# Macaron block on one core: row maxima of three heads moved into the feed-forward, their turns later, score banks apart

## Chip, cores and metric

The kernel runs on one core of one Trainium2 chip. The metric is the device time of one execution in microseconds (us). Three runs took 3427.9, 3429.25 and 3438.38 us, median 3429.25 us. Engines are named as in the profile: PE is TensorE, PEld its weight load, DVE VectorE, ACT ScalarE, POOL GpSimd, SP the queue that issues most transfers. A bank is one of the eight parts of PSUM, the memory that PE writes its results to; a bank holds 128 x 512 numbers of 32 bits.

## What is computed

Four sequences (B = 4) of T = 1024 rows and D = 512 columns pass through half a feed-forward, attention, and half a feed-forward again. Cut to what matters:

```python
def ffn(x):                                # H = 2048
    gate, up = split(x @ ternary(w_gate_up).T)
    h = silu(gate) * up
    h = h * rsqrt(mean(h * h) + eps)
    return h @ ternary(w_proj).T

def attention(x):                          # 32 query heads, 8 key heads, 16 wide
    Q, K, V = heads of x @ Wq.T + bq, x @ Wk.T + bk, x @ Wv.T + bv
    Q, K = rope(Q), rope(K)
    w = softmax(Q @ K.T / sqrt(16))        # four query heads share a key head
    return (w @ V) @ Wo.T + bo

x = x + 0.5 * ffn(layernorm(x))
x = x + attention(layernorm(x))
x = x + 0.5 * ffn(layernorm(x))
```

The softmax subtracts each row's maximum. The kernel finds these maxima in a pass of its own, before the scores are made a second time for the exponential.

## The kernel before

**Stages.** The work of the four sequences is pipelined. After a first part that prepares weights, each b = 0 to 3 has a feed-forward stage (FFN b), an attention stage (att b), and between att b and the next FFN a short stage of projections. FFN b doesn't work on sequence b alone: it takes three blocks of 512 rows, from feed-forwards that are due, last halves of older sequences ("z" blocks, whose rows are stored) and first halves of newer ones. A last FFN of two blocks ends the kernel. All stages touched here are under a manual schedule: each engine carries out its instructions in the order in which the program writes them.

**The feed-forward chunk** (`chunks`, L312). A block of 512 rows has 16 chunks of 128 hidden columns, so FFN b has 48 chunks; hc is the chunk's number in its block, n in the stage. A chunk runs in this order:

- `hidden` (L199): ACT widens the next weights (L100); PE makes `gu` twice in eight matmuls each (L211); ACT silu (L221); DVE `h` (L223); POOL `sq` and `acc` (L231, L235), the squares for the norm; ACT `high` (L237). `rest()`, called later, has DVE make `low` = h - high (L239).
- `project` (L251): `po` of the chunk two earlier, first for two of the four row tiles; then the call to attention, which is the subject here (see below); then the other two row tiles.
- After a block's last chunk: `factors` (L259) sums the squares on PE, POOL raises them to the power -0.5 (`inv`), DVE halves that (`half`, L277). `end` (L280) then adds `po` times `half` onto x (L288), which empties the four `po` banks; the first two x in one chunk, the other two in the next. It falls at hc = 1 and 2 of the next block, since `project` lags by two. At the stage's end all four x stand in a row.
- `rest()`; at even hc from 4 to 10 DVE normalises a row tile for the next block, with the root of its variance from POOL, and PE turns it one chunk later; steps noted for this hc (`later`, loads of x among them).

**The maxima.** Attention needs, for each of its 8 groups g (four query heads and one key head), 64 maxima; one is a 128 x 512 tile of scores, made by two matmuls of 32 rows each (`sm`, L1079) and reduced along its columns by DVE (`pm`, L1088). Four such, one from each head, run side by side on the four row groups of PE; I call this a four. The feed-forward takes one four in a chunk at most. `early` (L1133) decides it by a share of the stage: EARLY = 188 of a b's 512 maxima are done in FFN b, one four in every chunk from n = 2 (n = 5 for b = 0) to 47, less in total where the stage begins late: 184 for b = 1 to 3 and 172 for b = 0. The rest are done in attention, where each of the 128 steps takes three of them beside two pairs of score tiles, and some steps four (`more`, L1219 and L1236): 19 steps for b = 0 and 7 for each other b.

**The turn.** When a group's 64 maxima are there, `subtract_maxima` (L1097) collects them and puts a function `turn` on a list: PE transposes the maxima (`pmT`, L1113), DVE copies them (`mrow`, L1115), POOL writes them to memory (`d_m`, L1117), and for g = 0 POOL at once loads them back in another layout with four transfers (`mT`, L1130), which wait for `d_m` to land. The `early` call of the next chunk runs it, just ahead of that chunk's four. For b = 1 to 3 these are chunks 18 and 34, for b = 0 chunks 21 and 37. Chunk 18 and 34 (hc = 2) are also those in which the second half of the last block's `end` runs.

**Banks.** In the feed-forward tag `gu` has four banks (0 to 3), shared by `gu`, maxima, `pmT`, `pq` and the turned tiles; `po` has four (4 to 7, the four row tiles in 4, 7, 6 and 5). In attention the scores `s` have two pairs, banks 0 and 1 and banks 2 and 3; the maxima `sm` have 4, 6 and 5, the output `o` has 7. A bank that changes hands waits for the last reader of what was there.

Of the kernel before, what the change touches and what calls it, by code (L numbers as in the profile page):

```python
# [36 lines left out]
def tile_macaron_block(  # L37
# [103 lines left out]
    class FeedForward:  # L141
# [10 lines left out]
        def __init__(self, blocks, label, beside=None, begin=1):  # L152
            self.blocks, self.label, self.beside, self.begin = blocks, label, beside, begin
            self.order = [(k, hc) for k in range(len(blocks)) for hc in range(HC)]
            self.inputs, self.pos, self.accs, self.weights = {}, {}, {}, {}
            self.narrow = {}
            self.later = []
            self.first = tc.tile_pool(name=f"x{label}", bufs=1, reuse_waits="tile")
            self.even = self.first.__enter__()

# [98 lines left out]
        def factors(self, k):  # L259

            label = f"{self.label}_{k}"
            pq = self.ps.tile([P, 4], F32, tag="gu", name=f"pq_{label}")
            for i in range(4):
                for n, acc in enumerate(self.accs[k]):
                    nc.tensor.matmul(
                        pq[:, i : i + 1],
                        lhsT=acc[:, i * P : (i + 1) * P],
                        rhs=ones,
                        start=(n == 0),
                        stop=(n == len(self.accs[k]) - 1),  # L270
                    )
            ms = small.tile([P, 4], F32, tag="ms", name=f"ms_{label}")
            nc.vector.tensor_scalar(ms, pq, 1.0 / H, RMS_EPS, ALU.mult, ALU.add)
            inv = small.tile([P, 4], F32, tag="inv", name=f"inv_{label}")
            inverse_root(inv, ms, 4)
            half = small.tile([P, 4], F32, tag="half", name=f"half_{label}")
            nc.vector.tensor_scalar(half, inv, 0.5, None, ALU.mult)  # L277
            return half

        def end(self, k, half, some=range(4)):  # L280
# [31 lines left out]
        def chunks(self):  # L312
            last = len(self.order) - 1
            due, ends = [], []
            for n, (k, hc) in enumerate(self.order):
                if self.beside is not None:
                    places.piece()
                parts, rest = self.hidden(k, hc)
                if ends:
                    self.end(*ends.pop(), [2, 3])  # L320
                due.append((k, hc, parts))
                behind = due.pop(0) if len(due) > self.LAG else None
                if behind is not None:
                    self.project(*behind, [0, 1])
                if n == last:
                    rest()
                if self.beside is not None:
                    self.beside(self.ps, (n - self.begin) / (last - 1 - self.begin))
                if behind is not None:
                    self.project(*behind, [2, 3])  # L330
                    if behind[1] == HC - 1:
                        half = self.factors(behind[0])
                        self.end(behind[0], half, [0, 1])
                        ends.append((behind[0], half))
                if n < last:
                    rest()
                if k + 1 < len(self.blocks) and 4 <= hc < 12 and hc % 2 == 0:
                    for turn in self.normalize(k + 1, [hc // 2 - 2], self.wp, self.ps, "gu"):
                        self.later.append((hc + 1, turn))
                for step in [step for step in self.later if step[0] == hc]:  # L340
                    self.later.remove(step)
                    step[1]()

            for i in range(4):
                for behind in due:
                    self.project(*behind, [i])
                if i == 1:
                    half = self.factors(k)
            self.end(k, half)
            for _, step in self.later:  # L350
                step()
# [516 lines left out]
    class Attention:  # L868
# [18 lines left out]
        TOTAL = HKV * ITEMS * G  # L887
        READY = (HKV - 1) * STEPS - 5
        FIRST = 3
        EARLY = (3 * ITEMS - 1) * G  # L890

        def __init__(self, b):
            self.b = b


            self.d_q = dram.tile([D, 2, T], F32, tag="d_q", name=f"d_q_{b}", bufs=2)
            self.d_k = dram.tile([2, KV, 2, T], F32, tag="d_k", name=f"d_k_{b}", bufs=2)
            self.d_o = dram.tile([HQ, 2, HD, T], F32, tag="d_o", name=f"d_o_{b}", bufs=2)
            self.aT, self.after, self.when = {}, [], 0
            self.counts, self.turns = [0] * G, [0] * HKV  # L900
            self.pm, self.mT, self.mrows = {}, {}, {}
            self.early_rows = None
            self.rows, self.xTs, self.made = {}, {}, {}
            self.turning = []

        def weights_in(self):
            aux = places.at["out", self.b][2].bitcast(F32)
# [156 lines left out]
        def maxima(self, j, ps, bufs, passes):  # L1064

            g, n = divmod(self.counts[j], self.ITEMS)
            self.counts[j] += 1
            i, half = divmod(n, 2)
            q, *k = places.at["m", self.b, g]
            if g not in self.pm:  # L1070
                self.pm[g] = ring.tile([P, NT, G, 2], F32, tag="pm", name=f"pm_{self.b}_{g}")
            pm = self.pm[g]
            tag = "sm" if bufs < 4 else "gu"
            s = ps.tile([P, 512], F32, tag=tag, name=f"sm_{self.b}_{g}_{j}_{n}", bufs=bufs)
            at = slice(j * SLOT, (j + 1) * SLOT)

            def step(part):
                if part < 2:
                    nc.tensor.matmul(  # L1079
                        s,  # L1080
                        lhsT=q[at, i * P : (i + 1) * P],
                        rhs=k[part][at, half * 512 : (half + 1) * 512],
                        start=(part == 0),
                        stop=(part == 1),
                    )

            def end():
                nc.vector.tensor_reduce(pm[:, i, j, half : half + 1], s, AX.X, ALU.max)  # L1088
                self.turns[g] += 1
                if self.turns[g] == G * self.ITEMS:  # L1090
                    self.subtract_maxima(g, ps, bufs)
                    places.done(("m", self.b, g))

            passes.append(step)
            return end

        def subtract_maxima(self, g, ps, bufs):  # L1097

            b = self.b
            m = small.tile([P, NT, G], F32, tag="m", name=f"m_{b}_{g}", bufs=2)  # L1100
# [5 lines left out]
                mst[:, :, 1, :].bitcast(F32R), by_head, mst[:, :, 0, :], ALU.subtract  # L1106
            )
            rows = G * 2 * NT
            tag = "sm" if bufs < 4 else "gu"

            def turn():
                pt = ps.tile([P, 512], F32, tag=tag, name=f"pmT_{b}_{g}", bufs=bufs)
                nc.tensor.transpose(pt[:rows, :P], mst.rearrange("p j r i -> p (j r i)"), ident)  # L1113
                mrow = small.tile([rows, P], F32R, tag="mrow", name=f"mrow_{b}_{g}", bufs=2)
                nc.vector.tensor_copy(mrow, pt[:rows, :P])  # L1115
                self.mT[g] = dram.tile([rows, P], F32, tag="d_m", name=f"d_m_{b}_{g}", bufs=HKV)
                nc.gpsimd.dma_start(self.mT[g], mrow.bitcast(F32))  # L1117
                if g == 0:
                    self.maxima_in(g, ring, 1)
# [13 lines left out]
        def early(self, ps, share):  # L1133

            for at, kind, g in (
                (0.0, "m", 1),
                (0.3, "m", 2),
                (0.5, "s", 0),  # L1140
                (0.7, "m", self.FIRST),
                (0.8, "s", 1),
            ):
                if share >= at:
                    places.load((kind, self.b, g))
            if self.turning:
                self.turning.pop(0)()
            if sum(self.counts) + G <= min(share, 1.0) * self.EARLY:
                passes, ends = [], []
                for e in range(G):  # L1150
                    ends.append(self.maxima(sum(self.counts) % G, ps, 4, passes))
                together(passes, ends)

        def heads(self, keep):
# [6 lines left out]
        def run(self, keep, wp, ps):  # L1161
# [3 lines left out]
            def scores(g, qh, kc, pair, passes):  # L1165

                name = f"{b}_{g}_{qh}_{kc}_{pair}"
                s = ps.tile([P, 2, 512], F32, tag="s", name=f"s_{name}", bufs=2)
                keys, queries = slice(kc * P, (kc + 1) * P), slice(qh * 512, (qh + 1) * 512)
                q, *k = places.at["s", b, g]  # L1170

# [50 lines left out]
            for n in range(HKV * self.STEPS):  # L1222
# [26 lines left out]
                if late is not None:  # L1249
                    weigh(*late)  # L1250
                if turn is not None:
                    turn()
                late = g, qh, kc, es
            weigh(*late)
            places.done(("s", b, HKV - 2))
# [48 lines left out]
    def stage(b):  # L1304
        return FeedForward(
            blocks[b],
            f"{b}",
            beside=at[b].early if b < B else None,
            begin=1 if b > 0 else 4,
        )  # L1310

# [57 lines left out]
```

## Time and profile before

The profiled execution took 3426.07 us, its span is 3424.3 us, and the mean granted clock of PE is 0.983. Starts and lengths of stages by the windows of the trace, in us:

| stage | from | to | length | PE busy |
|---|---|---|---|---|
| FFN 0 | 314.2 | 636.1 | 321.9 | 316.3 |
| att 0 | 636.1 | 976.0 | 339.9 | 332.2 |
| FFN 1 | 1060.3 | 1385.1 | 324.8 | |
| att 1 | 1385.1 | 1718.2 | 333.1 | |
| FFN 2 | 1802.1 | 2121.9 | 319.8 | |
| att 2 | 2121.9 | 2454.9 | 333.0 | |
| FFN 3 | 2539.9 | 2867.2 | 327.3 | |
| att 3 | 2867.2 | 3197.7 | 330.5 | |
| FFN 4 | 3237.3 | end | 187.0 | |

A line of a timeline has the start, the length of the group, the engine, the source line, the operation, output<-inputs, shapes and how many instructions the group holds; in brackets stands the idle time of that engine just before, and what ended it. A line of a window has its bounds, its length, then busy time and count of PE, PEld, DVE, ACT and POOL, the granted clock of PE (1 is full speed), the busy share of the DMA engines and GB/s.

### The profile page before, as it was taken

The numbers are of one execution on the slowest core, as the hardware profiler recorded it, in microseconds if no ns is written. First come the engines' busy times: TensorE is split into PE (matmuls) and PEld (weight loads), VectorE is DVE, ScalarE is ACT, GpSimd is POOL, SyncE is SP. The second block draws the span as 40 slices with busy tenths as digits, with TensorE's granted clock in tenths as the row PEclk, the third lists the DMA queues.
The fourth block names the chain that finished last, engine by engine and source line by source line (L and its number), as shares of the span: only waits on it lengthen the run. The fifth ranks groups of instructions, "written<-read, shape, count | busy, mean of one in ns | idle before, by whom it ended". The sixth has DMA issues, their size and how long they took to land. (4 is left out here: it accounts for less than half of the span.)

```text
span 3424.3 us, 57120 instructions
## 1 busy us (share of the span) xinstructions
PE 3312.7 (97%) x22744; PEld 2147.2 (63%) x22744; DVE 2181.3 (64%) x3626; ACT 1765.4 (52%) x2346; POOL 950.3 (28%) x927
## 2 busy tenths in 40 slices
PE   5998999999999999999999999999999999999999
PEld 4777777544467777444477776444577775444687
DVE  7965666677636666777366666777256666775243
ACT  5742333577733333687713334778523335787343
POOL 2653343100123333100043333000243332010244
PEclk8999999999999999999999999999999999999999
DMA  3533222122323223123132221232231221322111
GB/s 117 157 97 103 61 76 79 40 94 91 105 60 97 78 65 101 57 99 101 65 89 81 88 79 56 75 98 91 74 106 52 78 91 54 96 92 77 32 45 56
DMA packets 211691, 278.47 MB, mean 81 GB/s; under 512 B 27616, under 2 KB 156640, under 8 KB 211424
## 3 DMA queue, kind: packets, MB, share of 16 engines
q1 hardware_dynamic: 201632, 263.26, 24.7%
q0 software_dynamic: 9792, 11.56, 1.4%
q8 instruction: 179, 2.93, 0.4%
q14 instruction: 88, 0.72, 0.1%
HBM read 216.01 MB, written 58.72 MB: 80 GB/s over the span
## 5 line engine op out<-in xcount | busy, mean ns | idle before, releaser
L1088 DVE TENSOR_REDUCE pm<-sm 128x1 f32<-128x512 f32 x2048 | 1284.6, 683 | 371.0 <-PE sm L1079 367.2
L1187 ACT ACTIVATE e<-s 128x1024 f32<-128x1024 f32 x1024 | 997.5, 1022 | 324.0 <-PE s L1176 321.2
L1079 PE MATMUL sm<-p_m,p_m 32*128 32x512 f32 x4096 | 769.2, 440 | 22.0 <-DVE pm L1088 11.4
L211 PE MATMUL gu<-xT,guT 128*128 128x512 f32 x1792 | 710.3, 396 | 13.3 <-ACT guT L100 12.5
L211 PE MATMUL gu<-xL,guT 128*128 128x512 f32 x1792 | 703.6, 393 | 0.3 <-DVE xL L139 0.3
L1176 PE MATMUL s<-p_s,p_s 32*128 32x512 f32 x4096 | 679.7, 437 | 0.0
L1176 PEld LDWEIGHTS s<-p_s,p_s 32*128 32x128 f32 x4096 | 317.4, 185 | 450.5 <-ACT e L1187 427.1
L1197 PE MATMUL o<-e,vs 128*32 128x512 f32 x4096 | 553.8, 613 | 1.8 <-ACT e L1187 1.8
L1079 PEld LDWEIGHTS sm<-p_m,p_m 32*128 32x128 f32 x4096 | 354.9, 185 | 122.3 <-DVE h L223 54.8
L1176 PE MATMUL s<-mT,ones_r 2*128 2x512 f32 x2048 | 417.3, 398 | 2.8 <-DMA mT<-d_m 2.8
L231 POOL TENSOR_TENSOR sq<-h 128x512 f32<-128x512 f32 x210 | 218.7, 1042 | 708.2 <-DVE h L223 708.0
L211 PEld LDWEIGHTS gu<-xT,guT 128*128 128x128 f32 x1792 | 340.0, 190 | 90.3 <-ACT guT L100 14.2
L221 ACT ACTIVATE sg<-gu 128x512 f32<-128x512 f32 x224 | 134.1, 599 | 497.1 <-PE gu L211 497.1
L223 DVE TENSOR_TENSOR h<-sg,gu 128x512 f32<-128x512 f32 x224 | 153.7, 686 | 368.9 <-PE gu L211 350.9
L211 PEld LDWEIGHTS gu<-xL,guT 128*128 128x128 f32 x1792 | 340.1, 190 | 70.2 <-DVE xL L139 0.7
L251 PE MATMUL po<-w_pT,high 128*128 128x512 f32 x896 | 371.9, 415 | 0.6 <-DVE x L288 0.6
L251 PE MATMUL po<-w_pT,low 128*128 128x512 f32 x896 | 351.8, 393 | 0.1
L237 ACT CAST high<-h 128x512 fp32r<-128x512 f32 x224 | 139.0, 620 | 342.1 <-DVE h L223 320.9
L235 POOL TENSOR_TENSOR acc<-acc,sq 128x512 f32<-128x512 f32 x205 | 276.4, 1348 | 16.0
L100 ACT CAST guT<-g 128x512 fp32r<-128x512 bf16 x448 | 274.8, 613 | 8.2 <-ACT guT L100 5.8
L251 PEld LDWEIGHTS po<-w_pT,high 128*128 128x128 f32 x896 | 168.3, 188 | 99.4 <-issue 65.5
L1176 PEld LDWEIGHTS s<-mT,ones_r 2*128 2x128 f32 x2048 | 198.5, 186 | 31.6 <-DMA mT<-d_m 4.5
(147 smaller groups left out, 3060.9 us busy)
## 6 DMA issues: line engine op xcount, KB each, us to landing
g<-d_guT SPq DMA_DIRECT2D x448, 128.0 KB
p_m<-d_k SPq DMA_DIRECT2D x56, 512.0 KB
p_s<-d_k SPq DMA_DIRECT2D x56, 512.0 KB
d_o<-oT SPq DMA_DIRECT2D x64, 256.0 KB
p_m<-d_q SPq DMA_DIRECT2D x28, 512.0 KB
p_s<-d_q SPq DMA_DIRECT2D x28, 512.0 KB
x<-in_L_attn_x_dram SPq DMA_DIRECT2D x32, 256.0 KB
w<-in_L_ffn_w_gate_up_dram SPq DMA_DIRECT2D x32, 256.0 KB
```

The costliest lines, as they stand in the source:

```text
L100: nc.scalar.copy(w, t)
L211: nc.tensor.matmul(pg, lhsT=self.weights[k, hc][part][:, c, :], rhs=xp[:, c, :], start=(c == 0 and low == 0), stop=(c == DC - 1 and low == 1),
L223: nc.vector.tensor_tensor(h, sg, gu[1], ALU.mult)
L231: nc.gpsimd.tensor_tensor(sq, h, h, ALU.mult)
L235: nc.gpsimd.tensor_tensor(acc, acc, sq, ALU.add)
L237: nc.scalar.copy(high, h)
L251: nc.tensor.matmul(self.pos[k][i], lhsT=h[:, i * P : (i + 1) * P], rhs=w_pT[hc], start=(hc == 0 and n == 0), stop=(hc == HC - 1 and n == 1),)
L1079: nc.tensor.matmul(s, lhsT=q[at, i * P : (i + 1) * P], rhs=k[part][at, half * 512 : (half + 1) * 512], start=(part == 0), stop=(part == 1),)
L1088: nc.vector.tensor_reduce(pm[:, i, j, half : half + 1], s, AX.X, ALU.max)
L1176: nc.tensor.matmul(s[:, e, :], lhsT=k[part][at, keys] if part < 2 else ones_r[at, :], rhs=(q if part < 2 else self.mrows[g])[at, queries], ...
L1187: nc.scalar.activation(w, s, AF.Exp, scale=1.0 / HD**0.5)
L1197: nc.tensor.matmul(o[j * SLOT : (j + 1) * SLOT, :], lhsT=vs[:, kc, g, :], rhs=es[j // 2][:, j % 2, :], start=(kc == 0), stop=(kc == NT - 1),)
```

## The change

- The feed-forward takes all 192 maxima of groups 0, 1 and 2 (EARLY = 192, 48 fours) in every FFN b < 4, and attention the other 320. There is one four in every chunk from n = `begin` (1, or 4 for b = 0) to n = 46 and none in the last chunk, n = 47. What is short of 48 is made up by a second four at the end of some chunks, behind `rest()` and the `later` steps: chunks 14 and 30 for b = 1 to 3; 14, 30, 46, 42 and 40 for b = 0.
- No attention step takes a fourth maximum any more.
- A waiting turn runs at the end of a chunk with hc = 3 or 13 and no longer in `early`: group 0's in chunk 19, group 1's in chunk 35. Group 2's turn runs in attention's step 0, as before.
- The root takes 4 times the mean square, so that POOL's result is `half` itself, and DVE's copy (16 instructions in the whole kernel) is gone.
- The two pairs of score banks have tags of their own, `s0` and `s1`, used in turn. By the built order `s0` has banks 0 and 1, the maxima 2, 4 and 3, `s1` 5 and 6, `o` 7. At attention's start the first scores and the first maximum thus use former `gu` banks; the second maximum waits for the first x of the block's end, the second pair of scores for the last.

```diff
+            short = Attention.EARLY // G - (len(self.order) - 1 - begin)
+            spare = [n for n, (k, hc) in enumerate(self.order[:-1]) if hc == 14]
+            spare += [len(self.order) - n for n in (6, 8, 10, 4, 12)]
+            self.twice_in = spare[:short] if beside is not None else []
...
-            nc.vector.tensor_scalar(ms, pq, 1.0 / H, RMS_EPS, ALU.mult, ALU.add)
-            inv = small.tile([P, 4], F32, tag="inv", name=f"inv_{label}")
-            inverse_root(inv, ms, 4)
+            nc.vector.tensor_scalar(ms, pq, 4.0 / H, 4.0 * RMS_EPS, ALU.mult, ALU.add)
             half = small.tile([P, 4], F32, tag="half", name=f"half_{label}")
-            nc.vector.tensor_scalar(half, inv, 0.5, None, ALU.mult)
+            inverse_root(half, ms, 4)
...
-                if self.beside is not None:
-                    self.beside(self.ps, (n - self.begin) / (last - 1 - self.begin))
+                if self.beside is not None and n < last:
+                    self.beside.early(self.ps, (n - self.begin) / (last - 1 - self.begin))
...
+                if n in self.twice_in:
+                    self.beside.four(self.ps)
+                if self.beside is not None and self.beside.turning and hc in (3, 13):
+                    self.beside.turning.pop(0)(self.ps, 4)
...
-        EARLY = (3 * ITEMS - 1) * G
+        EARLY = FIRST * ITEMS * G
...
-            if self.turning:
-                self.turning.pop(0)()
-            if sum(self.counts) + G <= min(share, 1.0) * self.EARLY:
+            if share >= 0.0:
+                self.four(ps)
+
+        def four(self, ps):
+
+            if sum(self.counts) < self.EARLY:
                 passes, ends = [], []
-                for e in range(G):
-                    ends.append(self.maxima(sum(self.counts) % G, ps, 4, passes))
+                for j in range(G):
+                    ends.append(self.maxima(j, ps, 4, passes))
                 together(passes, ends)
...
-                s = ps.tile([P, 2, 512], F32, tag="s", name=f"s_{name}", bufs=2)
+                s = ps.tile([P, 2, 512], F32, tag=f"s{self.turn_of_s}", name=f"s_{name}")
+                self.turn_of_s = 1 - self.turn_of_s
```

More of the change, by code (lines that the diff above doesn't have):

```diff
@@ L904, in __init__ @@
             self.turning = []
+            self.turn_of_s = 0
         def weights_in(self):
@@ L1090, in end @@
                 if self.turns[g] == G * self.ITEMS:
-                    self.subtract_maxima(g, ps, bufs)
+                    self.subtract_maxima(g)
                     places.done(("m", self.b, g))
@@ L1095, in maxima, with subtract_maxima @@
             return end
-        def subtract_maxima(self, g, ps, bufs):
+        def subtract_maxima(self, g):
             b = self.b
@@ L1108, in subtract_maxima, with turn @@
             rows = G * 2 * NT
-            tag = "sm" if bufs < 4 else "gu"
-            def turn():
+            def turn(ps, bufs):
+                tag = "sm" if bufs < 4 else "gu"
                 pt = ps.tile([P, 512], F32, tag=tag, name=f"pmT_{b}_{g}", bufs=bufs)
@@ L1251, in run @@
                 if turn is not None:
-                    turn()
+                    turn(ps, 3)
                 late = g, qh, kc, es
@@ L1307, in stage @@
             f"{b}",
-            beside=at[b].early if b < B else None,
+            beside=at[b] if b < B else None,
             begin=1 if b > 0 else 4,
```

## The prediction

> **What bounds the kernel now.** I read the page first (busy time, slices), then stages, and inside them chunks, steps, turns and boundaries by time of start. The page:
>
> ```profile
> PE   5998999999999999999999999999999999999999
> ...
> DVE  7965666677636666777366666777256666775243
> ...
> L1088 DVE TENSOR_REDUCE pm<-sm 128x1 f32<-128x512 f32 x2048 | 1284.6, 683 | 371.0 <-PE sm L1079 367.2
> ```
>
> From the third slice on, PE is busy at nine tenths everywhere and DVE at five to seven. So a moved instruction saves nothing by itself; what counts is whether PE stands still beside it. One maximum costs DVE 0.68 us wherever it runs.
>
> A feed-forward chunk with one four (four maxima) in FFN 0, begun by the first `gu` matmul:
>
> ```profile
> 617.79 0.40 PE L211 MATMUL gu<-xT,guT 128*128 128x512 f32 x1
> ...
> 623.18 2.48 DVE L1088 TENSOR_REDUCE pm<-sm 128x1 f32<-128x512 f32 x4 [0.78 <-PE sm L1079]
> ...
> 624.14 0.40 PE L211 MATMUL gu<-xT,guT 128*128 128x512 f32 x1
> ...
> 625.59 0.68 DVE L239 TENSOR_TENSOR low<-h,high 128x512 fp32r<-128x512 f32 x1
> ```
>
> The period is 624.14 - 617.79 = 6.35. Chunks of the same stage without a four take 5.44, so a plain four costs 0.91, PE time alone: its reduces run on beside the next chunk's eight-matmul groups.
>
> Attention steps, by the first matmul of `o`, and the reduces in two of them:
>
> ```profile
> 1414.85 1.06 PE L1197 MATMUL o<-e,vs 128*32 128x512 f32 x8
> ...
> 1417.44 1.06 PE L1197 MATMUL o<-e,vs 128*32 128x512 f32 x8
> ...
> 1420.62 1.06 PE L1197 MATMUL o<-e,vs 128*32 128x512 f32 x8
> ```
>
> ```profile
> 1416.62 1.89 DVE L1088 TENSOR_REDUCE pm<-sm 128x1 f32<-128x512 f32 x3 [0.48 <-PE sm L1079]
> ...
> 1419.21 2.61 DVE L1088 TENSOR_REDUCE pm<-sm 128x1 f32<-128x512 f32 x4 [0.71 <-PE sm L1079]
> ```
>
> Steps with three maxima take 2.37 and 2.59 in turn, 2.48 on average; the one with four took 3.18. A maximum is thus dearer in attention (0.70) than in a plain four (0.91 / 4 = 0.23). The question is which of the moved maxima get the cheap place.
>
> **Part 1: steps with four maxima go.** Before, 40 attention steps take a fourth maximum: 19 for b = 0, 7 for each other b. Four are step 0 of a stage, counted with the boundary below. The other 36 last 3.17 to 3.21 nearly all; over their neighbours 0.72 on average. Gain 36 x 0.72 = **25.9**. The cover for the remaining three is there already: DVE needs 1.89 of 2.48. All maxima end at step 106 before and after, so the tail of the stage doesn't move.
>
> **Part 2: doubled fours.** To hold 48 fours without the last chunk, 11 chunks get a second one: two in each of b = 1 to 3, five in b = 0. It stands at the chunk's end, behind `low`. No row of before shows that. In the chunk above: its first matmuls take the four `gu` banks that the first four's reduces are still reading; the last is free at 623.18 + 2.48 = 625.66, so PE ends at about 626.2. The second four's first reduce follows `low`: 626.27 to 626.95. The next chunk's first `gu` needs that bank: 627.0 instead of 624.14, **2.85** each, 11 x 2.85 = 31.4. From below the price is a plain four's 0.91 (10.0 in all); that would need free banks. A gain is excluded: the eight matmuls are real PE work.
>
> The clock comes on top. Two neighbouring clock windows at a turn of the maxima (part 3):
>
> ```profile
> 1181.86:1185.27 3.41, 2.39 (x13) 1.33 (x12) 2.79 (x6) 1.14 (x2) 2.76 (x3) 1.00 0.75 184
> 1185.27:1188.69 3.42, 3.42 (x9) 2.67 (x8) 2.23 (x4) 0.00 (x0) 0.13 (x1) 0.50 0.99 264
> ```
>
> Columns: window, then busy PE, PEld, DVE, ACT, POOL, granted clock, DMA share, GB/s. PE idle for 1.02 of 3.41 was followed by a window at half speed; so was the one at 635.73, idle for 0.93 (part 4). Counting a 32-row matmul as a quarter of a full one, windows with up to 0.36 of PE's time at work were followed by 0.50 and from 0.37 by 1.00 (one exception). A doubled four's stalls, laid at every phase of the window, come under that line in 38% of phases; a slow window costs about 1.5. So 0.57 each, **6.3** in all; bounds 0 and 17.
>
> The Trainium skill ("TensorE: Matmul & The Clock Gate", Part 1) says that the clock falls after at least one idle window of about 3.4 us. In the rows above it fell after one idle microsecond of 3.41; by the page these 6.3 would be nothing, by the rows they stay.
>
> **Part 3: the turns.** Six turns of g = 0 and 1 in b = 1 to 3, and two in b = 0, stand in an `early` call now. In b = 1:
>
> ```profile
> 1181.72 0.27 PE L1113 MATMUL pmT<-ident,mst 128*64 128x128 f32 x1
> ...
> 1182.21 1.40 DVE L288 SCALAR_TENSOR_TENSOR x<-po,half,x 128x512 f32<-128x512 f32 x2
> 1183.53 0.27 DVE L1115 CAST mrow<-pmT 64x128 fp32r<-64x128 f32 x1
> ...
> 1183.85 0.73 PE L1079 MATMUL sm<-p_m,p_m 32*128 32x512 f32 x5 [1.02 <-DVE mrow L1115]
> ```
>
> `mrow` stands on DVE behind the block end's two x (1.40), so the bank comes free late, PE waits 1.02, and the clock halves. The turn's chunk and the next take 8.88 + 7.72 and 9.31 + 7.31 (b = 1), 8.70 + 6.36 and 8.69 + 6.33 (b = 2), 9.20 + 7.44 and 9.75 + 6.85 (b = 3), against 6.70 + 6.44 for the same two in FFN 0, which turns elsewhere; that one's own turns cost 0.89 and 0.53. The excesses sum to 19.1. After, each turn stands at the end of chunk 19 or 35, no block end beside it; waiting for the first reduces it costs about 0.3: 8 x 0.3 = 2.4. Gain **16.7**, bounds 0 (it stalls as much at the new place) and 19.1.
>
> Behind g = 0's turn POOL issues four `mT` loads that wait for `d_m` to land:
>
> ```profile
> 1192.17 2.05 POOL L1130 DMA_DIRECT2D mT<-d_m  x4 [6.77 <-DMA d_m<-mrow]
> ...
> 463.30 2.06 POOL L1130 DMA_DIRECT2D mT<-d_m  x4 [1.51 <-DMA d_m<-mrow]
> ```
>
> In the new place these head off chunk 20's `sq`, `acc` and the root of the row scales on POOL, behind which DVE's normalised rows and the next `h` queue, for whose delay PE's maxima wait. By my timing a wait up to 2.2 is hidden; at 6.5 to 6.95, as b = 1 to 3 had it, `h` is 4.8 late plus a cold window, 6.3 each. The long waits stood among output stores (DMA share 0.75 and 0.99 above), which chunk 19 does not have, so I take the short one with a small charge: 3 x 1 = **3**, bounds 0 and 19.
>
> **Part 4: banks and boundary.** Before, in FFN 0's end:
>
> ```profile
> 635.51 0.17 DVE L277 TENSOR_SCALAR half<-inv 128x4 f32<-128x4 f32 x1 [1.15 <-POOL inv L104]
> ...
> 635.72 2.73 DVE L288 SCALAR_TENSOR_TENSOR x<-po,half,x 128x512 f32<-128x512 f32 x4
> ...
> 637.84 0.49 PE L1079 MATMUL sm<-p_m,p_m 32*128 32x512 f32 x1 [0.82 <-DVE x L288]
> ```
>
> The four x empty the `po` banks one by one. With no four in the last chunk and no `half` copy, x begins at about 634.97 and ends at 637.7. The first scores and the first maximum now lie in `gu` banks and start at once, but the second pair of scores takes the banks of the last x for all b: it starts at 637.76, PE having waited about 1.3. I get the first `o` at 641.5 against 641.9 now: 4 x 0.35 = **1.4** gain, four fewer plain fours and step 0's fourth maximum included. The half-speed windows behind the four boundaries (10.24, 13.65, 3.41, 10.24 us of them, 16 us lost) I leave as they are: the wait in front remains. Bounds -8 and +8, half of that loss either way.
>
> The other `half` copies (0.17 and a gap each) at block ends, in the first stage and at the tail: **2** gain, bounds 0 and 3.
>
> **Part 5: fours from chunk 1.** In b = 1 to 3 chunk 1 gets a four, on a stage's first chunks:
>
> ```profile
> 1071.03 0.50 PE L211 MATMUL gu<-xT,guT 128*128 128x512 f32 x1 [3.06 <-ACT guT L100]
> ```
>
> There is no `po` work yet to cover it. The fourth maximum's bank waits for `h` of chunk 1, which ends at 1072.2; chunk 2's `gu` waits for the first reduce and starts at 1073.5 instead of 1071.03: 2.5 x 3 = **7.5**, and in two of the three a cold window more: **2.8** (bounds 0 and 4.5). From below: 0.91 x 3. In b = 0 chunk 4 gets one, plain: **0.9**.
>
> **Sum.** Gains 25.9 + 16.7 + 1.4 + 2 = 46.0. Losses 31.4 + 6.3 + 3 + 7.5 + 2.8 + 0.9 = 51.9. Net 5.9 slower on the profiled execution's 3426.07 (span 3424.3), which lies 3.2 under the median 3429.25 of the runs shown: 3429.25 + 5.9 = **3435**, plus 0.17%. About 0.3% (10.3 us) is what a measurement of this kernel can tell from no change.
>
> **Rivals.**
> 1. *The clock forgives* (faster): no slow window after doubled fours and chunk 1 (-9.1), no POOL charge (-3), boundaries 8 better: 5.9 - 20 = 14 faster, **3415**. For it: the line lies between 0.36 and 0.37 of a window, and the stalls straddle it. Against: all four boundaries cooled before, and a wait stays in front of the second pair.
> 2. *`mT` loads block POOL* (slower): mechanism and place as in part 3, deciding from a landing over 2.2 us after the issue. Price up to 6.3 in each of b = 1 to 3: 19 instead of 3, **3451**. For it: three waits of 6.5 to 6.95; against: 1.51 where no stores ran.
> 3. *Doubled fours cost a plain four*, if banks turn out free: 31.4 + 6.3 becomes 10.0, **3407**. Against: the same four banks in the chunk above are read until 625.66.
>
> That the maxima don't move at all is excluded: the built order has 192 in each such stage and 320 in attention, with the same 15334 rows of PE instructions and 16 fewer of DVE.
>
> **Chances.** Forecast (within 0.3%) 0.45; rival 1 0.15 and rival 3 0.05, both faster: 0.20; rival 2 0.20, and 0.15 for boundaries and clock at their bad bounds: slower 0.35. The range reaches from rival 1 to rival 2 with the bad boundary in part, 3414 to 3456; rival 3 is left out.
>
> **What would show it.** Part 1: steps all at 2.4 to 2.6. Part 2: chunks 14 and 30 (in b = 0 also 40, 42, 46) at about 9.2 instead of 6.35, `gu` after `pm`. Part 3: chunks 19 and 35 at 6.7, 18 and 34 too; POOL's wait for `d_m` under 2.2. Part 4: x begins about 0.75 earlier against the last `po`, `s` of the second pair waits for x. Part 5: chunk 2's first `gu` waits 2.5 for a reduce. Wrong, if PE finds other work in the doubled chunks, or attention begins warm.

## The result and the profile after

| | before | after |
|---|---|---|
| median of 15 runs each, us | 3431.53 (3416.49 to 3438.38) | 3439.77 (3427.04 to 3449.11) |
| span of the profiled execution | 3424.3 | 3436.6 |
| mean granted clock | 0.983 | 0.984 |

The ratio of the times is 1.0034, 95% interval 1.0021 to 1.0046: the change costs 7 to 16 us. That lies around the line of 0.3% which the prediction drew; 3435 had been forecast from 3429.25, a plus of 0.17%. Before ran again with every set of experiments, and all ratios below are to it. Where the intervals of two changed kernels overlap or meet, their ratios alone don't tell them apart, and the text goes by the chunks and steps of their traces; each trace shows one execution.

The page of the changed kernel, three rows:

```profile
L1098 DVE TENSOR_REDUCE pm<-sm 128x1 f32<-128x512 f32 x2048 | 1282.1, 684 | 367.2 <-PE sm L1089 365.7
...
L217 PE MATMUL gu<-xT,guT 128*128 128x512 f32 x1792 | 718.1, 401 | 15.7 <-DVE pm L1098 7.9
...
L1190 PE MATMUL s<-p_s,p_s 32*128 32x512 f32 x4096 | 678.0, 438 | 5.0 <-DVE x L293 5.0
```

The 2048 reduces take what they took. Two waits of PE in these rows are new: the `gu` groups stood 7.9 behind reduces (the doubled fours and chunk 1), and the scores 5.0 behind x (the second pair, four times 1.24). The rest of the price doesn't show as idle time, since a matmul that waits on the way counts as busy.

The doubled four at the end of chunk 14 in FFN 0, by the timelines of PE and DVE:

```profile
410.86 0.39 PE L217 MATMUL gu<-xT,guT 128*128 128x512 f32 x1
...
416.32 2.48 DVE L1098 TENSOR_REDUCE pm<-sm 128x1 f32<-128x512 f32 x4 [0.80 <-PE sm L1089]
...
417.36 2.23 PE L1089 MATMUL sm<-p_m,p_m 32*128 32x512 f32 x8
...
419.41 2.48 DVE L1098 TENSOR_REDUCE pm<-sm 128x1 f32<-128x512 f32 x4
...
420.15 0.50 PE L217 MATMUL gu<-xT,guT 128*128 128x512 f32 x1 [0.56 <-DVE pm L1098]
```

The eight matmuls of the second four take 2.23 where the first four's take 0.75: each of its four banks comes free only when a reduce has read it. The next `gu` waits for the first reduce of the second four. The chunk takes 420.15 - 410.86 = 9.29 against 6.40 for its neighbours. What the clock makes of it, by the windows of the same place (after the length: busy PE, PEld, DVE, ACT, POOL; granted clock, DMA share, GB/s):

```profile
417.62:421.03 3.41, 2.64 (x12) 1.39 (x12) 3.41 (x6) 0.00 (x0) 0.44 (x1) 1.00 0.15 38
421.03:424.44 3.41, 3.41 (x10) 2.67 (x9) 0.86 (x2) 0.85 (x2) 0.00 (x0) 0.50 0.01 2
```

A window in which PE counts as busy for 2.64 of 3.41, most of it 32-row matmuls that wait, is followed by one at half speed, and the next chunk takes 8.09 instead of 6.49. This befell 4 of the 11 doubled fours. The Trainium skill's "TensorE: Matmul & The Clock Gate" (Part 1) ties the fall to at least one idle window; as before the change, no window here was idle, so the rows hold.

Where the 12.3 us between the two profiled executions lie, beside the forecast's terms (us, after minus before; chunks by the starts of their first `gu`, steps by the first matmul of `o`):

| place | forecast | measured |
|---|---|---|
| 11 doubled fours, their waits | +31.4 | +32.7 |
| the clock behind them | +6.3 | +6.4 |
| chunks 1 and 2 of b = 1 to 3 | +10.3 | +9.6 |
| chunk 4 of b = 0 | +0.9 | +0.9 |
| turns away from the block's end | -16.7 | -15.1 |
| `mT` loads on POOL (chunks 20 and 21) | +3 | +4.6 |
| fourth maxima gone, steps 20 to 100 | -11.5 | -9.1 |
| last chunk to step 20, fourth maxima in it | -15.8 | -29.6 |
| `half` copies; all other chunks | -2 | +4.1 |
| end of attention, steps 100 to 127 | 0 | +3.6 |
| first part, FFN 0's first chunks, projections | 0 | +4.1 |
| sum | +5.9 | +12.2 |

The rows hold for these two executions. Those that depend on half-speed windows (the second and third, the start and the end of attention) can differ in another.

### The profile page after: what moved, and what is told of

The parts are those of the page before. It is cut to its first block, busy times and chain, and to the rows that moved or that the text cites. A ratio compares the mean times of both kernels' runs of the same rounds, so it can differ in the third digit from the quotient of the medians.

```text
span 3436.6 us, 57095 instructions
## 1 busy us (share of the span) xinstructions
PE 3325.9 (97%) x22744; PEld 2152.6 (63%) x22744; DVE 2179.2 (63%) x3610; ACT 1761.5 (51%) x2346; POOL 948.4 (28%) x927
## 3 DMA queue, kind: packets, MB, share of 16 engines
q8 instruction: 179, 2.93, 0.4%
## 5 line engine op out<-in xcount | busy, mean ns | idle before, releaser
L1089 PE MATMUL sm<-p_m,p_m 32*128 32x512 f32 x4096 | 760.1, 437 | 12.2 <-ACT sg L227 5.3
L217 PE MATMUL gu<-xT,guT 128*128 128x512 f32 x1792 | 718.1, 401 | 15.7 <-DVE pm L1098 7.9
L1190 PEld LDWEIGHTS s<-p_s,p_s 32*128 32x128 f32 x4096 | 309.1, 184 | 458.0 <-ACT e L1201 429.8
```

The lines of the kernel that those rows point to most:

```text
L217: nc.tensor.matmul(pg, lhsT=self.weights[k, hc][part][:, c, :], rhs=xp[:, c, :], start=(c == 0 and low == 0), stop=(c == DC - 1 and low == 1),
L1089: nc.tensor.matmul(s, lhsT=q[at, i * P : (i + 1) * P], rhs=k[part][at, half * 512 : (half + 1) * 512], start=(part == 0), stop=(part == 1),)
L1190: nc.tensor.matmul(s[:, e, :], lhsT=k[part][at, keys] if part < 2 else ones_r[at, :], rhs=(q if part < 2 else self.mrows[g])[at, queries], ...
```

## The experiments

Each set ran on one chip, with the kernel before beside it.

**1. Addresses.** The untouched chunks of the last feed-forward take 5.50 in the changed kernel and 5.44 before. With `inv` gone, the pool it lay in is 128 bytes per partition smaller, and all tiles allocated later move down by as much. `e1` keeps the bytes:

```diff
+            inv = small.tile([P, 4], F32, tag="inv", name=f"inv_{label}")
             half = small.tile([P, 4], F32, tag="half", name=f"half_{label}")
             inverse_root(half, ms, 4)
```

> The change with one addition: the 128 bytes per partition of the tile inv stay allocated (never written), so that every later tile keeps its address of before. In the profile of the changed kernel the chunks of the last feed-forward, which the change does not touch, take 5.50 us instead of 5.44. Theory 1 (addresses: the shift by 128 bytes makes some matmuls 5 to 11 ns longer): the untouched chunk is back at 5.44, and the kernel is 8 to 11 us faster than the changed one, ratio to before about 1.000. Theory 2 (that profile's execution or chip was slower by itself): no difference to the changed kernel, ratio about 1.003.

> The kernel before with only the halving copies taken away (inv no longer allocated, later tiles 128 bytes lower). My prediction's term: 2 us faster, ratio 0.9994. Addresses theory: 2 us gained and 9 to 11 lost, ratio 1.002 to 1.003, the untouched chunk of the last feed-forward at 5.50 us instead of 5.44. Theory of a slower execution: ratio 0.9994, chunk at 5.44.

Starts of chunks 20 and 21 of the last feed-forward, in the changed kernel and in `e1`:

```profile
3359.32 0.39 PE L217 MATMUL gu<-xT,guT 128*128 128x512 f32 x1
...
3364.82 0.39 PE L217 MATMUL gu<-xT,guT 128*128 128x512 f32 x1
```

```profile
3364.29 0.39 PE L217 MATMUL gu<-xT,guT 128*128 128x512 f32 x1
...
3369.73 0.39 PE L217 MATMUL gu<-xT,guT 128*128 128x512 f32 x1
```

5.50 and 5.44. All 14 profiles agree: 5.50 in the six kernels with the shift (after, `e2`, `e5`, `e6`, `e7`, `e9`), 5.44 in the eight without. That it goes with the shift and not with the execution is shown; how is not. But its price was overrated: over all chunks that differ by less than 0.13, the changed kernel loses 4.1 us to `e1`, and `e2` 4.6 to before. The ratios, 1.0027 (1.0013 to 1.0041) for `e1` and 0.9993 (0.9979 to 1.0006) for `e2`, can't tell so little; they exclude that the shift is the whole loss.

**2. One part alone.** `e3` is before with the two tags for scores, `e4` before with the turns at the end of chunks with hc 3 or 13.

> The kernel before with only the scores' banks allotted apart (tags s0 and s1). My prediction's term, without the last chunk's four: about 0, ratio 1.000, attention beginning at half speed after all four boundaries as before. Rival read from the changed kernel's trace: after two of its four boundaries the clock stays whole, so 8 to 14 us faster, ratio 0.996 to 0.998.

> The kernel before with only the turns of groups 0 and 1 put at the end of a chunk with hc 3 or 13. My prediction's terms: 16.7 us gained, 3 lost by the mT loads on POOL, ratio 0.996; chunks 18 and 34 at 6.70, chunk 21 (two after the turn) up to 8.5 instead of 7.05 where POOL waits for d_m over 2.2 us. Rival: the stall only moves to the new place, ratio 1.000.

`e3`: 1.0004 (0.9993 to 1.0016). Apart alone, the banks bring nothing: the stretch from the last chunk's first `gu` to step 20 is 299.7 over the four stages, 299.5 before, with 37.5 us at half speed in both.

`e4`: 0.9979 (0.9964 to 0.9994), about 7 us faster; 14 were forecast. Two things took the rest. Chunk 18 takes 7.42 or 7.43 and not 6.70: with fours from n = 2 the group's last four falls into chunk 17, and the small operations that collect its maxima stand on DVE ahead of the block end's x. The changed kernel is done two chunks earlier, and chunk 18 takes 6.67 to 6.69. And POOL, in chunk 20 of b = 2:

```profile
1938.42 2.06 POOL L1132 DMA_DIRECT2D mT<-d_m  x4 [3.60 <-DMA d_m<-mrow]
...
1939.90 2.21 DVE L239 TENSOR_TENSOR low<-h,high 128x512 fp32r<-128x512 f32 x1
...
1945.01 0.73 PE L1081 MATMUL sm<-p_m,p_m 32*128 32x512 f32 x5 [1.42 <-DVE h L223]
```

The four loads keep POOL from `sq` and `acc`, which now run beside `low`; `low` takes 2.21 instead of 0.68, `h` comes late, PE waits 1.42. Chunk 21 takes 8.91 here, and the next 7.71 at half speed.

**3. The doubled fours.** `e5` sets `self.twice_in = []`; attention takes the 44 maxima as fourth ones again. `e6` puts pairs of maxima into twice as many chunks:

```diff
+            spare = [12, 14, 28, 30, 46, 44, 42, 40, 38, 36]
+            self.twice_in = spare[: 2 * short] if beside is not None else []
...
+        def pair(self, ps):
+
+            a = 0 if self.counts[0] == self.counts[2] else 2
+            self.four(ps, (a, a + 1))
```

> The changed kernel without the 11 doubled fours; their 44 maxima go back to attention as fourth maxima of a step. Theory 1 (a doubled four costs 2.85 by its wait for the banks, and 0.57 by the clock): 37.7 us gained, 26 to 29 given back, so 9 to 12 faster than the changed kernel, ratio to before 1.000. Rival (a doubled four costs little more than a plain one, and the loss lies elsewhere): 10 gained and 26 to 29 given back, ratio 1.008.

> The changed kernel with 22 pairs of maxima at chunk ends in place of the 11 doubled fours, the same 192 maxima in each feed-forward. By the chunk at 617.79 of before, a pair waits for the second of the first four's reduces and the next gu for the third: about 0.95 us a pair, 21 in all. Theory 1 (the price of a doubled four is its wait for the banks): 31 + 6 become 21 with no cold window, 14 to 17 us faster than the changed kernel, ratio to before 0.998 to 0.999. Rival (the price is the work on PE and DVE, which stays): ratio 1.003.

`e5`: 1.0005 (0.9990 to 1.0021), 10 us under the changed kernel, as the first theory has it and against the rival's 1.008. (The two intervals meet at 1.0021; in the trace the chunks in question are back at 6.35 to 6.41.) In b = 0 it pays for something new: turns in chunks 19 and 35 stand in the chunk of their group's last four there, and take 8.84 and 8.86.

`e6`: 1.0006 (0.9988 to 1.0025), also 10 us under the changed kernel, where 14 to 17 were forecast. The intervals overlap a little, so the chunks have to show it. A pair in chunk 14 of FFN 1:

```profile
1162.52 0.39 PE L216 MATMUL gu<-xT,guT 128*128 128x512 f32 x1
...
1167.98 2.48 DVE L1097 TENSOR_REDUCE pm<-sm 128x1 f32<-128x512 f32 x4 [0.80 <-PE sm L1088]
...
1169.01 1.04 PE L1088 MATMUL sm<-p_m,p_m 32*128 32x512 f32 x4
...
1169.98 0.19 PEld L216 LDWEIGHTS gu<-xT,guT 128*128 128x128 f32 x1 [0.36 <-DVE pm L1097]
1169.98 0.50 PE L216 MATMUL gu<-xT,guT 128*128 128x512 f32 x1
```

7.46 instead of 6.40 and 0.09 in the next chunk: 1.15 a pair, 25 in all instead of 39. Four banks are nearly enough now: the weight load of `gu` (PEld) waits 0.36 for the third reduce, and no chunk behind the first three of a stage runs at half speed (13.6 us did in the changed kernel). So the price of a doubled four is mostly the wait for banks: the same maxima are cheaper when fewer stand behind each other.

**4. The turns again.** `e7` is the changed kernel with `hc == 13` in place of `hc in (3, 13)`.

> The changed kernel with turns at chunk ends with hc 13 alone: group 0's goes from chunk 19 to chunk 29 and group 1's from 35 to 45, where no rows are normalised. Theory (POOL's mT loads delay the root that DVE and the next chunks wait for): chunk 21 at 7.05 instead of 7.84 to 8.44, 4 us faster than the changed kernel, ratio to before 1.002. Rival (the delay of chunk 21 has another cause): chunk 21 unchanged, ratio 1.003.

1.0023 (1.0004 to 1.0041). Chunk 21 is back at 7.03 to 7.06, so the turn with POOL's loads was its delay. But group 0's turn now stands in chunk 29, ahead of the doubled four in chunk 30, which takes 10.05 to 10.33 instead of 9.26 to 9.29: most of the delay only moved, and the time can't be told from the changed kernel's.

**5. The terms together.** `e8` has pairs, turns at hc 13, `begin=2` for b = 1 to 3, and `inv`'s bytes. `e11` adds a fourth maximum in four steps of two stages:

```diff
+                if b in (1, 2) and n in (24, 30, 37, 43):
                     sides[1] = (2 * first, 2 * first + 1)
```

> Pairs in place of doubled fours, turns at hc 13 alone, the fours of b = 1 to 3 from chunk 2 and not chunk 1 (two pairs more in each of these stages), and the addresses of before kept. By my terms: 17 for the pairs, 4 for the turns, 10.3 for chunk 1 less 5.7 for six more pairs, so about 25 us faster than the changed kernel, ratio to before 0.995 to 0.996. If the terms don't add (waits move elsewhere): 0.998 or more.

> The version with pairs, turns at hc 13, chunk 1 free and the addresses of before, and with a fourth maximum in four attention steps (24, 30, 37, 43) of b = 1 and 2, so that all maxima are done one step earlier there. Theory: the wait for the last group's mT at step 110 of b = 2 (4.8 and 3.5 us steps, in other runs up to ten steps at half speed) goes; 8 x 0.72 = 5.8 lost and 4 to 10 gained, ratio to before 0.994 to 0.996. Rival: mT lands no earlier, since something else holds it: 0.9975.

`e8`: 0.9958 (0.9942 to 0.9975), median 3415.78: 14 us faster than before and 26 than the changed kernel, with 25 forecast. It beats both kernels. In the profiles the feed-forward stages give 24.1 of the 25.5 us between these two; attention's start is 11 longer than in the changed kernel, its end and the projections 9 shorter. `e11`: 0.9956 (0.9942 to 0.9971), no difference to `e8` that can be measured, though the wait it aimed at fell to 0.43 (7 below): steps 100 to 127 of b = 2 take 66.7 against 70.0.

**6. The start of attention.** In the changed kernel this stretch gained 29.6 where I had 15.8. `e9` is the changed kernel with one tag for the scores again, `e10` before with `n < last` for the four, `e12` before with `n > 0` ahead of the condition for a fourth maximum.

> The changed kernel with the scores' pairs under one tag again (by the built order s in banks 0 to 3 and the maxima in 4 to 6, as before), all else kept. In the changed kernel's trace the stretch from the last chunk's first gu to step 20 of attention got 15 us shorter over the four boundaries than the removed fourth maxima explain. Theory A (the banks apart keep PE at work and the clock up): that is lost, the kernel 8 to 15 us slower than the changed one, ratio to before 1.006 to 1.008. Theory B (the last chunk without a four does it, the banks nothing): ratio 1.003 as the changed kernel, boundaries as short as there.

> The kernel before with no four in the last chunk; these four maxima of each b are taken as fourth maxima of attention steps behind step 20 (20 and 8 such steps instead of 19 and 7, and longer). By my terms 16 x 0.72 = 11.5 lost and 4 x 0.91 less in the last chunk. Theory A (banks decide): the stretch from the last chunk to step 20 is 0.9 shorter each, 8 us slower in all, ratio 1.002. Theory B (the last chunk's four decides): that stretch is 2.5 to 4 shorter each and the first steps run at full clock in two of four, ratio 1.000.

> The kernel before without the fourth maximum in attention's step 0 (it is taken in a later step, one more of these per b). Banks apart alone (0 us over the four boundaries) and the last chunk without a four alone (3 us) did not give the changed kernel's shorter starts of attention. Theory C (step 0's fourth maximum loads DVE behind the four x, and keeps PE waiting and the clock down): the stretch from the last chunk's first gu to step 20 gets 8 to 12 us shorter over the four stages, half-speed time there falls from 37 us to about 20, 2.9 us lost in later steps, ratio 0.998. Rival (only the parts together do it): stretch shorter by less than 3 us in all, ratio 1.000 to 1.001.

| kernel | ratio (interval) | last chunk to step 20, four stages | of it at half speed |
|---|---|---|---|
| before | 1 | 299.5 | 37.5 |
| `e3` banks apart alone | 1.0004 (0.9993 to 1.0016) | 299.7 | 37.5 |
| `e10` last chunk free alone | 1.0024 (1.0008 to 1.0041) | 296.2 | 37.5 |
| `e12` step 0 with three, alone | 1.0026 (1.0011 to 1.0042) | 299.2 | 40.9 |
| `e5` changed, fourth maxima kept | 1.0005 (0.9990 to 1.0021) | 290.6 | 23.8 |
| changed | 1.0034 (1.0021 to 1.0046) | 270.0 + 14.4 | 10.2 |
| `e9` changed, banks together | 1.0057 (1.0039 to 1.0076) | 272.7 + 14.4 | 17.0 |
| `e1` changed, addresses kept | 1.0027 (1.0013 to 1.0041) | 278.6 + 14.4 | 30.7 |

14.4 stands for the 20 fourth maxima that these kernels don't have there (step 0's four are in the forecast's 1.4). No part alone shortens the stretch by more than 3.3; theory C of `e12` falls. (`e10` takes a fourth maximum in 23 and 11 steps, not in 20 and 8 as I wrote; the 16 more of them made steps 20 to 100 12.2 longer, as 11.5 was expected.) In `e9` it stays short without the banks apart, so they aren't needed for it. The gain needs several parts at once, and its size changes with the half-speed windows from one kernel to the next (`e8`, with the same start, has 34.2 us of them). An estimate from these rows: take 14.4 and half of the half-speed time saved (the clock is 0.50 there) from the gain, and the seven kernels with the changed start (changed, `e1`, `e9` and, outside the table, `e6`, `e7`, `e8`, `e11`) keep 1.3 to 3.2 us, near the forecast's 1.4. By this the rest of the gain is the clock. Which pair of parts is enough was not tried, and why the windows fall in one kernel and not in another is open.

The times of `e9` spoke for theory A, its stretch for B. Its profile (span 3457.3) has ten steps at half speed, 34.1 us, at the end of b = 2, where the changed kernel's has 6.8; the same ten steps stand in the profiles of `e4` and `e6`, with the banks together and apart. The interval of `e9` overlaps the changed kernel's too. I don't count its ratio as shown for the banks.

**7. The end of attention.** `e12` lost 9 us by something that no theory named. With three maxima in step 0 all are done in step 107 and not 106, and the last group's `mT` comes later than its scores. The first scores of the last group in b = 2: `e12`, before, and `e11`, where all are done a step earlier:

```profile
2429.55 1.10 PE L1176 MATMUL s<-mT,ones_r 2*128 2x512 f32 x2 [1.92 <-DMA mT<-d_m]
```

```profile
2410.95 1.33 PE L1176 MATMUL s<-mT,ones_r 2*128 2x512 f32 x2 [1.90 <-DMA mT<-d_m]
```

```profile
2406.05 0.70 PE L1195 MATMUL s<-mT,ones_r 2*128 2x512 f32 x2 [0.43 <-DMA mT<-d_m]
```

Steps 100 to 127 take 71.3, 70.5, 74.5 and 66.0 (b = 0 to 3) in `e12`, 67.3, 67.1, 70.9 and 66.0 before, 66.8, 66.4, 66.7 and 66.0 in `e11`. Waits of 1.90 to 2.16 us (in `e12` for b = 0 to 2, before for b = 2) go with 70.5 to 74.5 us for these steps, where stages without such a wait take 66 to 67: half-speed windows of 3.41 to 17.07 us stand behind the waits.

## Why the prediction was right, point by point

The direction holds, and most of the mechanism; the size is twice the forecast: +0.34% (0.21 to 0.46) measured, +0.17% forecast. The forecast's own band, "within 0.3%", was just left by the middle of the interval. That the sum came so near is partly luck: in the profiles the start of attention came out 13.8 us better than forecast and the other rows together 20.1 worse.

- *Part 1, fourth maxima.* Right: 9.1 of 11.5 where it can be read apart from the boundary.
- *Part 2, doubled fours.* Right in wait, bank and size (2.97 against 2.85 each), and in the clock: 4 of 11 against 38% (5 of 11 in `e1`; eleven chunks don't test the share closely). Rival 3 (banks free) is refuted by the second four's 2.23 and by `e6`. This is the term that makes the change lose: it is dearer (39 us) than the fourth maxima that it replaces (26 by forecast).
- *Part 3, turns.* Right: 15.1 of 16.7, and `e4` shows the gain alone. The new place costs 0.4 each, not 0.3.
- *Rival 2, POOL.* It happened in part. The waits were 3.63, 2.93, 3.19 and 1.50, the delays 1.75, 0.88, 1.14 and 0.79. So the short wait that part 3 took for all came once in four. "Hidden up to 2.2" was wrong, since 1.50 cost 0.79. The price of 6.3 for a wait of over 6 was not tested, because none was over 3.7. The link I had missed is `low`. In the changed kernel, chunk 20 of b = 1:

```profile
1215.29 2.05 POOL L1140 DMA_DIRECT2D mT<-d_m  x4 [2.93 <-DMA d_m<-mrow]
...
1217.36 1.05 POOL L237 TENSOR_TENSOR sq<-h 128x512 f32<-128x512 f32 x1
...
1217.45 1.52 DVE L245 TENSOR_TENSOR low<-h,high 128x512 fp32r<-128x512 f32 x1
1218.49 1.63 POOL L241 TENSOR_TENSOR acc<-acc,sq 128x512 f32<-128x512 f32 x1
...
1221.88 0.73 PE L1089 MATMUL sm<-p_m,p_m 32*128 32x512 f32 x5 [0.69 <-DVE h L229]
```

- *Part 4, boundary.* The wait was as forecast:

```profile
2145.10 2.72 DVE L293 SCALAR_TENSOR_TENSOR x<-po,half,x 128x512 f32<-128x512 f32 x4 [1.15 <-POOL half L104]
...
2147.88 0.50 PE L1190 MATMUL s<-p_s,p_s 32*128 32x512 f32 x2 [1.24 <-DVE x L293]
```

  (The first `o` before the change stands at 643.24 in the trace, not at 641.9: half speed begins at 639.1.) The failed step is "I leave as they are", said of the half-speed windows: they fell from 37.5 to 10.2 us in this profile, and the stretch gained 15.2 beyond the fourth maxima instead of 1.4, nearly twice the bound of 8. Rival 1's "boundaries better" came true in part (6.6 in `e1`), its "no slow window after doubled fours" did not.
- *`half`.* The term left out the shift of addresses, which costs 4.1 in the chunks of these profiles, more than the 2 that it was to gain. The times don't settle its sign: `e2` alone is at 0.9993 (0.9979 to 1.0006).
- *Part 5, chunk 1.* Right in the sum, 9.6 against 10.3, and in the two half-speed windows; without it (`e8`) chunks 1 and 2 of b = 2 and 3 are back at 5.33 + 6.53 and 5.94 + 6.49. The split was off: chunk 2 begins 5.3 later over the three stages, not 7.5, and chunk 2 itself, at half speed, is 4.3 longer, not 2.8. And the wait for a reduce is 0.58, not 2.5. In b = 1 the long wait is for ACT's `sg` in chunk 1, as PE waited for ACT before the change (3.06, for `guT`):

```profile
1081.89 0.50 PE L1089 MATMUL sm<-p_m,p_m 32*128 32x512 f32 x1 [2.11 <-ACT sg L227]
...
1083.92 0.80 PE L217 MATMUL gu<-xT,guT 128*128 128x512 f32 x1 [0.58 <-DVE pm L1098]
```

- *Not priced:* the end of attention. The change keeps step 106, but a stage's last `mT` stands so close that this stretch took 3.6 more here, and 269 to 281 us over the twelve kernels that keep step 106.

## What to carry to other kernels

A moved instruction is paid at its new place: before moving one, look who reads the bank that it will take and who wants that bank next; the same work in smaller portions, which fit the free banks, cost a third less for each maximum (1.15 for two, 3.55 for four). A turn or a copy that others wait for goes where nothing long stands ahead of it on its engine, and its loads go where that engine's later work isn't wanted soon. Change one part at a time: here gains of 15 and (by forecast) 26 us hid behind losses of 39 and 10, and the parts put together otherwise (`e8`) gave 0.4% to the other side.

## What the runs showed of the hardware

- Tiles moved by 128 bytes per partition make PE's stream longer in kernels that are otherwise the same: in the chunk above the first three matmuls of `gu` follow each other at 231 to 232 ns instead of 227, and those of `po` at 224 to 238. The cause is open.
- `low` (two inputs from SBUF) takes 0.68 alone; in the four chunks behind group 0's turn in the changed kernel, with POOL's last loads, `sq` and `acc` beside it, 1.46 to 2.25, and in three of the four `acc` 1.63 or 1.64 instead of 1.29. In all four `low` ends 0.55 or 0.56 after `sq` does (for b = 3 after `acc`), as if it had stood until then; why is not shown. The Trainium skill ("GPSIMD Engine Reference", 1. Specifications) says that GpSimd shares its SBUF interfaces with VectorE, with contention where a DVE instruction has two SBUF inputs; these rows agree.
- Half speed lasts. At the end of b = 2 three profiles (`e4`, `e6`, `e9`) stay at half clock for ten steps, 34.1 us, after the wait for `mT`, though PE is at work again (3.41 of 3.41 in each window of `e9`); of the others `e1` has 20.5 there, `e12` 17.1, the rest 6.8 or less. What decides it was not found. From 400 us of a profile to 10 us before its end, the time at half speed ranged from 31 us (`e11`) to 102 (`e9`).
